# Transposes of z, and of two tiles of the last batch, by 16-bit transfers in a planned attention and feed-forward kernel

## The chip, the cores and the metric

The kernel runs on one core of a Trainium2 chip. The metric is the device time of one execution in microseconds, as the median of several executions. The profile is of one further execution and gives the span from its first to its last instruction.

## What is computed

All data is float32. Eight batches of 512 rows by 256 columns go through two blocks. Cut to what matters:

```python
y  = layernorm(x)
y  = layernorm(y + attention(y, y, y, causal=True)) * g1 + beta1
y  = layernorm(y + attention(y, Z, Z))              * g2 + beta2     # Z: 64 rows of 256 per batch
y  = layernorm(y + relu(y @ w1 + b1) @ w2 + b2)     * g3 + beta3     # w1 256x1024, w2 1024x256
x  = x + y
u  = layernorm(x)
h  = silu(fp4(u) @ fp4(w_gate).T) * (fp4(u) @ fp4(w_up).T)           # 704 columns
x  = x + fp4(h) @ fp4(w_down).T
# fp4: blocks of 16 along the row, scaled by the block's maximum / 6, rounded to a 4-bit grid, scaled back
```

## The kernel before

A batch is four tiles of 128 rows. TensorE contracts over partitions, so y, z, the rounded u (`zq`) and the rounded h must each be turned before a product. There are two ways to turn a tile. By products: TensorE transposes it into a PSUM bank and ScalarE evicts the bank (`transposed`, L411; its transposes are line L419, and L1102 for the last columns of h). By transfers: ScalarE copies the float32 tile into two planes of 16-bit halves (L843 for y, r and zq, L1071 for h), SP writes the planes to DRAM (L849, L1077), and SP issues a transfer that transposes 16-bit elements back into SBUF (L854, L1082). `BY_PRODUCTS` says for which batches y0, r in cross-attention and r in the MLP are turned by products (4, 2 and 1 first batches); zq goes by transfers in every batch, h by transfers in all but the last batch, z by products in every batch.

No engine runs its instructions in program order. Each step is given to a `Plan` with an engine, a duration in microseconds, what it reads and writes, and the buffers that it takes. `Plan.order` runs a small list scheduler over these durations: whenever an engine is free, it takes, from the steps that are ready and whose buffers are free, the one with the least key. The key comes from `DUE`, a table of due times per batch and stage (0 self-attention, 1 cross-attention, 2 MLP, 3 gate and up products, 4 down products), carried back through the successors; `LOAD_EARLY` brings the loads of x and z forward, and `plan.push` moves the weights' rounding. The order that comes out is then emitted, so each engine's queue is fixed, SP's among them. A transfer's `lag` is the planned time from its issue to its landing.

Buffers are kinds with a number of homes (`several(name, count, shape)`); `share` gives a kind a quota out of another kind's homes. The names that matter below:

- `x`, `z`: a batch's inputs, loaded at L358 and L366; `y0`, `r`: the running rows.
- `zT`: the turned z, evicted at L867 with the factor 1/16; it is read at L883 by the products that make the cross-attention's scores, which ScalarE copies to `kq` (L896) and TensorE transposes once more (L900). The products with z as values are L927.
- `turned`: homes of the turned y0, r and zq (evicted at L831 when made by products). `zm`: staging of their 16-bit planes. For zq the same buffer is the mask of the rounding (L578 to L610), held from the maximum on.
- `h` (in `wide`), `hm`, `hqT`: the gated tile, its 16-bit planes, the turned tile; `hd` is the DRAM side. L597 is the absolute value within the rounding, L610 its last step.

The products by line: L767 self-attention scores, L800 its values, L961 and L981 the MLP, L1036 gate and up, L1116 down. L488 are the squares of a layernorm, and L503 and L458 its power -1/2 on POOL. For the last batch all four gated tiles are made first and the four down products follow:

```python
if b == B - 1:
    hs = [gate_up(t) for t in range(NT)]
    for t in range(NT):
        down(t, hs[t])
```

Of the kernel before, what the change touches and what calls it, by code (L numbers as in the profile page):

```python
# [12 lines left out]
U16 = mybir.dt.uint16  # L13
# [6 lines left out]
P = 128  # L20
# [20 lines left out]
TILED = 2.65  # L41

BY_PRODUCTS = (4, 2, 1)
LOAD_EARLY = 2191.0
DUE = [
    [-1877.0, 638.0, 1236.0, -86.0, 359.0],
    [-498.0, 1140.0, 299.0, -53.0, 352.0],
    [251.0, 920.0, -109.0, 452.0, 665.0],
    [2244.0, 599.0, -92.0, 754.0, 95.0],
    [1032.0, 759.0, 1302.0, 1127.0, 22.0],  # L50
    [818.0, -579.0, 119.0, -1108.0, 586.0],
    [771.0, -1583.0, 341.0, 621.0, 85.0],
    [127.0, -388.0, -430.0, -94.0, -1479.0],
    [-2334.0],
]


# [8 lines left out]
def act(cols, bias=False):  # L66
    return 0.06 + cols * 0.84e-3 + 0.19 * bias
# [193 lines left out]
def kernel(  # L261
# [43 lines left out]
    def several(name, count, shape):  # L305
        return [fixed(f"{name}_{k}", shape) for k in range(count)]


    plan = Plan(due=DUE)
    plan.kind("x", several("x", 6, [P, NT, D]))  # L310

    y0_homes = several("y0", 2, [P, NT, D + 2])

    z_homes = several("z", 8, [P, D + 2])
    plan.kind("y0", y0_homes)
    plan.kind("z", z_homes)
    plan.kind("zT", several("zT", 6, [P, ND, SZ]))
    plan.kind("turned", several("turned", 3, [P, ND, S]), ordered=False)
    plan.share("y0T", "turned", 1)
    plan.share("yT", "turned", 3, ordered=False)  # L320
    plan.share("zqT", "turned", 3)
    plan.kind("e", several("e", 1, [P, NT * (NT + 1) // 2 * P]))
    plan.kind("r", several("r", 3, [P, NT, D]))
    plan.kind("kq", several("kq", 4, [P, S // 2]))
    plan.kind("xp", several("xp", 6, [P, NT, SZ]))
    plan.kind("xpT", several("xpT", 3, [P, NT // 2 * P]))
    plan.kind("hT", several("hT", 8, [P, S]))
    plan.kind("zq", several("zq", 1, [P, NT, D]))
    plan.kind("zm", several("zm", 2, [P, NT * D]), ordered=False)
    plan.kind("wide", several("h", 8, [P, NI * P]), ordered=False)  # L330
    plan.share("h", "wide", 5)
    plan.share("hm", "wide", 3)
    plan.share("wq", "wide", 7)
    hqT_homes = several("hqT", 3, [P, NI * P])
    plan.kind("hqT", hqT_homes)

    hd_homes = [dram.tile([P, 2, NI * P], U16, tag=f"hd_{k}", name=f"hd_{k}") for k in range(3)]
# [2 lines left out]
    plan.kind("rest", [rest_home])  # L340
    zd_homes = [dram.tile([NT, P, 2, D], U16, tag=f"zd_{k}", name=f"zd_{k}") for k in range(4)]
    plan.kind("zd", zd_homes, ordered=False)
    plan.kind("ln", several("ln", 12, [P, 48]), ordered=False)
    plan.kind("q", several("q", 6, [P, 3, 64]), ordered=False)
    plan.kind("rt", several("rt", 7, [P, 4]), ordered=False)
    banks = [psum.tile([P, 512], F32, tag=f"bank{k}", name=f"bank_{k}") for k in range(8)]
# [78 lines left out]
    def norm_stats(v, view, pairs):  # L425

        s = plan.buf("ln")

        def st(t):
            return s.ap[:, 6 * t : 6 * t + 6]  # L430

        def mv(t):
            return s.ap[:, 24 + 2 * t : 26 + 2 * t]

        def variances(ts_):
            lo, hi = ts_[0], ts_[-1] + 1
            for t in ts_:
                nc.vector.bn_aggr(mv(t), st(t))
            nc.vector.tensor_scalar(
                s.ap[:, 32 + lo : 32 + hi],  # L440
                s.ap[:, 24:32].rearrange("p (t k) -> p t k", k=2)[:, lo:hi, 1], EPS, None, ALU.add,
            )

        for ts_ in pairs:
            lo, hi = ts_[0], ts_[-1] + 1
            for t in ts_:
                plan.op(
                    "DVE", 0.33, lambda t=t: nc.vector.bn_stats(st(t), view(t)),
                    reads=[(v, t)], writes=[(s, ("st", t))],
                )  # L450
            plan.op(
                "DVE", 0.1 + 0.09 * len(ts_), lambda ts_=ts_: variances(ts_),
                reads=[(s, ("st", t)) for t in ts_],
                writes=[(s, ("var", lo))] + [(s, t) for t in ts_],
            )
            plan.op(
                "POOL", 1.05,
                lambda lo=lo, hi=hi: nc.gpsimd.tensor_tensor(  # L458
                    s.ap[:, 36 + lo : 36 + hi], s.ap[:, 32 + lo : 32 + hi], mhalf[:, lo:hi], ALU.pow
                ),  # L460
                reads=[(s, ("var", lo))], writes=[(s, ("rstd", t)) for t in ts_],
            )
            plan.op(
                "DVE", 0.15,
                lambda lo=lo, hi=hi: nc.vector.scalar_tensor_tensor(
                    s.ap[:, 40 + lo : 40 + hi],
                    s.ap[:, 24:32].rearrange("p (t k) -> p t k", k=2)[:, lo:hi, 0],
                    -1.0, s.ap[:, 36 + lo : 36 + hi], ALU.mult, ALU.mult,
                ),
                reads=[(s, ("rstd", t)) for t in ts_] + [(s, t) for t in ts_],  # L470
                writes=[(s, ("shift", t)) for t in ts_],
            )
        return s

    def sums_stats(v, view, s):


        plan.op(
            "DVE", 0.08,
            lambda: nc.vector.tensor_scalar(  # L480
                s.ap[:, 24:28], s.ap[:, :4], -1.0 / D, None, ALU.mult
            ),
            reads=[(s, ("st", t)) for t in range(NT)], writes=[(s, t) for t in range(NT)],
        )
        for t in range(NT):
            plan.op(
                "ACT", 0.52,
                lambda t=t: nc.scalar.activation(  # L488
                    squares, view(t), AF.Square, bias=s.ap[:, 24 + t : 25 + t],
                    accum_out=s.ap[:, 28 + t : 29 + t],  # L490
                ),
                reads=[(v, t), (s, t)], writes=[(s, ("sq", t))],
            )
        plan.op(
            "DVE", 0.08,
            lambda: nc.vector.tensor_scalar(  # L496
                s.ap[:, 32:36], s.ap[:, 28:32], 1.0 / D, EPS, ALU.mult, ALU.add
            ),
            reads=[(s, ("sq", t)) for t in range(NT)], writes=[(s, "var")],
        )  # L500
        plan.op(
            "POOL", 1.05,
            lambda: nc.gpsimd.tensor_tensor(s.ap[:, 36:40], s.ap[:, 32:36], mhalf, ALU.pow),  # L503
            reads=[(s, "var")], writes=[(s, ("rstd", t)) for t in range(NT)],
        )
# [241 lines left out]
    def self_attention(b, xs):  # L747
# [13 lines left out]
        for k in range(NT):  # L761
            n = S - k * P
            sc = plan.buf("bank")

            def scores(k=k, n=n, sc=sc):
                for c in range(ND):
                    nc.tensor.matmul(  # L767
                        sc.ap[:, :n], yT.ap[:, c, ts(k, P)], yT.ap[:, c, k * P :],
                        start=(c == 0), stop=(c == ND - 1),
                    )  # L770

            plan.op(
                "PE", ND * pe(n), scores, reads=[(yT, c) for c in range(ND)], writes=[sc],
                takes=[e],
            )
            plan.op(
                "ACT", act(n, True),
                lambda k=k, n=n, sc=sc: nc.scalar.activation(

                    e.ap[:, ds(start[k], n)], sc.ap[:, :n], AF.Exp, scale=1.0 / 16.0  # L780
                ),
                reads=[sc], writes=[(e, k)], table="exp",
            )

            plan.op(
                "POOL", 0.35,
                lambda k=k: nc.gpsimd.affine_select(
                    out=e.ap[:, ds(start[k], P)], in_=e.ap[:, ds(start[k], P)],
                    compare_op=ALU.is_ge, fill=0.0, base=0, pattern=[[1, P]],
                    channel_multiplier=-1,  # L790
                ),
                writes=[(e, k)],
            )
# [66 lines left out]
    def cross_attention(b, r, zs):  # L860

        plan.stage = 1
        zT = plan.buf("zT")
        transposed(
            lambda: [zs.ap[:SZ, ts(c, P)] for c in range(ND)], [(zs, 0)], (zT, None),

            lambda pt: nc.scalar.activation(  # L867
                zT.ap, pt[:, : ND * SZ].rearrange("p (c k) -> p c k", c=ND),
                AF.Copy, scale=1.0 / 16.0,
            ),  # L870
            act(ND * SZ), 2,
        )
        yT = turned(r, "yT", b < BY_PRODUCTS[1], lambda t: r.ap[:, t, :])
        sc, nm, xp = plan.buf("bank"), plan.buf("rt"), plan.buf("xp")
# [18 lines left out]

        plan.op("PE", 1.05, products, reads=[yT, zT], writes=[keys])
        kq = plan.buf("kq")
        plan.op("ACT", act(S // 2), lambda: nc.scalar.copy(kq.ap, keys.ap[:, : S // 2]), reads=[keys], writes=[kq])  # L896

        def scores():
            for j in range(2):
# [47 lines left out]
    def mlp(b, r, xs):  # L947
# [8 lines left out]
        for f in range(NF):  # L956
            hp, h = plan.buf("bank"), plan.buf("hT")

            def product(f=f, hp=hp):
# [5 lines left out]

            plan.op("PE", ND * pe(S), product, reads=[yT, ready["w1"]], writes=[hp], takes=[h])
            plan.op(
                "ACT", act(S, True),
                lambda f=f, hp=hp, h=h: nc.scalar.activation(  # L969
                    h.ap, hp.ap, AF.Relu, bias=b1_sb[:, f : f + 1]  # L970
                ),
# [47 lines left out]
    def glu(b, xs, s):  # L1019
# [42 lines left out]
        def down(t, h):  # L1062
            plan.stage = 4
            m = fp4(h, lambda h=h: h.ap[:, :I], "hm", NBI)
            hqT = plan.buf("hqT")
            if b < B - 1:
                hd = plan.buf("hd")
                planes = lambda: m.ap[:, :I].bitcast(U16).rearrange("p (h k) -> p h k", h=2)
                plan.op(
# [65 lines left out]
            )  # L1135


        if b == B - 1:
            hs = [gate_up(t) for t in range(NT)]
            for t in range(NT):  # L1140
                down(t, hs[t])
        else:
            for t in range(NT):
                down(t, gate_up(t))
# [15 lines left out]
        "SP", 5.2, lambda: nc.sync.dma_start(w2_sb, w2.rearrange("(c p) d -> p c d", p=P)),  # L1160
        writes=[ready["w2"]],
    )
    plan.push = 2035.0
    weights()
    plan.push = 0.0
    for b in range(B):
# [38 lines left out]
```

## Time and profile before

| | us |
|---|---|
| median of three executions | 575.2 (574.42, 575.2, 576.3) |
| profiled execution, its own time | 576.26 |
| its span, first to last instruction | 574.5 |
| TensorE busy | 563.8 |
| VectorE busy | 447.8 |
| ScalarE busy | 361.8 |
| POOL busy | 62.2 |

Busy time is the union of an engine's instructions, so pipelined matmuls are not counted twice. The DMA engines were busy 45.4% of the span. In the chain of work that ended last each piece is followed back to what released it; an instruction's line is the line of the helper that emits it, and for transposes the tile's name after `ident` tells what is turned. The granted TensorE clock was 1.00 throughout.

### The profile page before, as it was taken

What the parts mean: (1) busy time and instruction counts of PE and PEld (TensorE: products, weight loads), DVE (VectorE), ACT (ScalarE), POOL (GpSimd) and SP (SyncE); (2) the same over time, 40 slices, a digit from 0 to 9 for tenths busy, and PEclk for the clock granted to TensorE, in tenths of its full rate; (3) what the DMA queues carried; (4) which work ended last, traced back from release to release, by engine and by line L of the source; (5) the groups of instructions that cost most, each with busy time, mean ns of one, the idle gap of its engine ahead of it and who ended that gap; (6) DMA issues with size and microseconds to landing.
All of it is one profiled execution on the core that took longest, in us unless ns stands there. A gap on an engine that the chain in (4) does not pass through costs nothing.

```text
span 574.5 us, 7037 instructions
## 1 busy us (share of the span) xinstructions
PE 563.8 (98%) x2209; PEld 391.2 (68%) x2209; DVE 447.8 (78%) x1125; ACT 361.8 (63%) x761; POOL 62.2 (11%) x93
## 2 busy tenths in 40 slices
PE   5999999999999999999999999999999999999997
PEld 2767584866747668658486667766765866877686
DVE  4789988869998865755259999978997656399892
ACT  4677869598887672791638558887845256364431
POOL 3521101011200120110101102210100000010000
PEclk9999999999999999999999999999999999999999
DMA  7770387246466513322023546585771421436501
GB/s 236 119 230 2 101 219 169 73 119 157 116 158 175 137 52 83 99 71 49 1 73 98 137 126 156 148 198 154 153 180 62 124 62 38 111 106 151 151 19 46
DMA packets 143220, 66.88 MB, mean 116 GB/s; under 512 B 107976, under 2 KB 142672, under 8 KB 143184
## 3 DMA queue, kind: packets, MB, share of 16 engines
q1 hardware_dynamic: 143184, 66.44, 45.4%
q8 instruction: 17, 0.28, 0.2%
q14 instruction: 19, 0.16, 0.1%
HBM read 10.42 MB, written 29.66 MB: 70 GB/s over the span
## 4 chain that ended last, share of the span: by engine, by line
PE 98%; ACT 1%; DMA 0%; SPq 0%; issue 0%; DVE 0%; ACTq 0%
PE bank L1036 27%; PE bank L981 19%; PE bank L961 19%; PE bank L1116 15%; PE bank L767 7%; PE bank L800 6%; PE bank L419 2%; PE bank L927 1%; PE bank L883 1%; DMA z<-in_ctx_dram 0%; ACT squares L488 0%; PE bank L900 0%; SPq L358 0%; ACT turned L831 0%; PE bank L1102 0%
## 5 line engine op out<-in xcount | busy, mean ns | idle before, releaser
L1036 PE MATMUL bank<-wgu,turned 128*128 128x352 f32 x512 | 157.5, 460 | 0.0
L1036 PEld LDWEIGHTS bank<-wgu,turned 128*128 128x128 f32 x512 | 96.3, 190 | 51.8 <-issue 1.7
L981 PE MATMUL bank<-w,hT 128*128 128x256 f32 x512 | 112.6, 379 | 0.0
L961 PE MATMUL bank<-turned,w 128*128 128x512 f32 x256 | 112.5, 593 | 0.0
L981 PEld LDWEIGHTS bank<-w,hT 128*128 128x128 f32 x512 | 97.0, 190 | 13.8
L1116 PE MATMUL bank<-wd,hqT 128*128 128x256 f32 x384 | 87.2, 380 | 0.0
L961 PEld LDWEIGHTS bank<-turned,w 128*128 128x128 f32 x256 | 48.2, 190 | 56.9 <-issue 51.7
L1116 PEld LDWEIGHTS bank<-wd,hqT 128*128 128x128 f32 x384 | 72.4, 190 | 14.2 <-issue 2.9
L503 POOL TENSOR_TENSOR ln<-ln,mhalf 128x4 f32<-128x4 f32 x32 | 37.7, 1180 | 352.0 <-DVE ln L496 352.0
L603 DVE SCALAR_TENSOR_TENSOR h<-h,h 128x704 f32<-128x704 f32 (+2 forms) x76 | 66.8, 883 | 3.8 <-ACT h L597 3.4
L488 ACT ACTIVATE squares<-r,ln 128x256 f32<-128x256 f32 x96 | 48.7, 508 | 32.0 <-DVE ln L480 29.7
L969 ACT ACTIVATE hT<-bank,cols 128x512 f32<-128x512 f32 x64 | 42.8, 681 | 21.7 <-PE bank L961 21.5
L1048 ACT ACTIVATE h<-bank 128x352 f32<-128x352 f32 x64 | 29.2, 460 | 36.4 <-PE bank L1036 32.5
L1071 ACT COPY h<-h 128x1408 uint16<-128x1408 uint16 x28 | 38.0, 1362 | 19.4 <-DVE h L610 17.9
L1055 DVE TENSOR_TENSOR h<-h,bank 128x352 f32<-128x352 f32 x64 | 32.4, 516 | 12.3 <-PE bank L1036 8.6
L992 DVE SCALAR_TENSOR_TENSOR r<-bank,r 128x256 f32<-128x256 f32 x32 | 13.5, 421 | 35.0 <-PE bank L981 34.7
L767 PE MATMUL bank<-turned 128*128 128x512 f32 (+3 forms) x128 | 39.8, 457 | 0.4 <-ACT turned L831 0.4
L597 ACT ACTIVATE h<-h 128x704 f32<-128x704 f32 (+2 forms) x38 | 29.7, 788 | 14.0 <-DVE h L591 13.9
L800 PE MATMUL bank<-y,e 128*128 128x258 f32 x160 | 36.8, 381 | 0.0
L800 PEld LDWEIGHTS bank<-y,e 128*128 128x128 f32 x160 | 30.1, 190 | 5.9 <-issue 1.0
L591 DVE SCALAR_TENSOR_TENSOR h<-h,q 128x704 f32<-128x704 f32 (+2 forms) x38 | 33.5, 883 | 0.2
L610 DVE TENSOR_TENSOR h<-h,q 128x704 f32<-128x704 f32 (+2 forms) x38 | 33.4, 879 | 0.2
(90 smaller groups left out, 639.9 us busy)
## 6 DMA issues: line engine op xcount, KB each, us to landing
zd<-zm SPq DMA_DIRECT2D x25, 512.0 KB, 3.0
hd<-h SPq DMA_DIRECT2D x30, 352.0 KB, 3.0
out_dram<-x SPq DMA_DIRECT2D x32, 128.0 KB, 1.7
x<-in_x_dram SPq DMA_DIRECT2D x7, 512.0 KB, 5.3
w<-in_L_xattn_w_dram SPq DMA_DIRECT2D x2, 1024.0 KB, 7.4
z<-in_ctx_dram SPq DMA_DIRECT2D x16, 64.0 KB, 4.6
zd<-h SPq DMA_DIRECT2D x2, 384.0 KB, 3.1
h<-in_L_ffn_w_down_dram SPq DMA_DIRECT2D x2, 352.0 KB, 4.2
```

Source lines behind the costliest of these rows:

```text
L488: lambda t=t: nc.scalar.activation(squares, view(t), AF.Square, bias=s.ap[:, 24 + t : 25 + t], accum_out=s.ap[:, 28 + t : 29 + t],),
L503: lambda: nc.gpsimd.tensor_tensor(s.ap[:, 36:40], s.ap[:, 32:36], mhalf, ALU.pow),
L591: lambda: nc.vector.scalar_tensor_tensor(blocks_of(view()), blocks_of(view()), TIE, each(rc()), ALU.mult, ALU.mult),
L603: lambda reverse=reverse, f=f: nc.vector.scalar_tensor_tensor(view(), mm(), LEAST, view(), ALU.max, f, reverse1=reverse),
L767: nc.tensor.matmul(sc.ap[:, :n], yT.ap[:, c, ts(k, P)], yT.ap[:, c, k * P :], start=(c == 0), stop=(c == ND - 1),)
L800: nc.tensor.matmul(av.ap[:, : D + 2], e.ap[:, ds(start[k] + (t - k) * P, P)], y0.ap[:, k, :], start=(k == 0), stop=(k == t),)
L961: nc.tensor.matmul(hp.ap, w1_sb[:, c, ts(f, P)], yT.ap[:, c, :], start=(c == 0), stop=(c == ND - 1),)
L969: lambda f=f, hp=hp, h=h: nc.scalar.activation(h.ap, hp.ap, AF.Relu, bias=b1_sb[:, f : f + 1]),
L981: nc.tensor.matmul(fp.ap[:, :D], hT[f].ap[:, ts(t, P)], w2_sb[:, f, :], start=(f == 0), stop=(f == NF - 1),)
L1036: nc.tensor.matmul(gp.ap[:, :HI], zT.ap[:, c, ts(t, P)], wgu[:, c, ds(j * I + n * HI, HI)], start=(c == 0), stop=(c == ND - 1),)
L1071: lambda: nc.scalar.copy(planes(), h.ap[:, :I].bitcast(U16).rearrange("p (k h) -> p h k", h=2)),
L1116: nc.tensor.matmul(op.ap[:, :D], hqT.ap[:, ts(c, P)], wd[:, c, :], start=(c == 0), stop=(c == NI - 1),)
```

## The change

- z is turned by transfers in all batches. ScalarE copies 64 rows of z into two 16-bit planes (`zpl`, five homes), SP writes them to DRAM (`zzd`, four homes) and SP issues the transposing transfer into `zT`. The factor 1/16 moves from the eviction of zT to the copy of `kq`.
- In the last batch, tiles 0 and 1 of h are turned by transfers, as in all other batches; tiles 2 and 3 stay with TensorE.
- Four planned durations take other values: the power on POOL, the squares, the causal selection on POOL and the relu on ScalarE.
- The numbers of homes and quotas change, and the due times, `LOAD_EARLY` and the push of the weights are new. With the durations they set the order of every queue.

```diff
-LOAD_EARLY = 2191.0
+LOAD_EARLY = 5413.0
 DUE = [
-    [-1877.0, 638.0, 1236.0, -86.0, 359.0],
-    [-498.0, 1140.0, 299.0, -53.0, 352.0],
...
+    [-2265.0, 403.0, 787.0, -473.0, 177.0],
+    [-532.0, 884.0, 23.0, -239.0, 262.0],
...
-    plan.kind("x", several("x", 6, [P, NT, D]))
+    plan.kind("x", several("x", 5, [P, NT, D]))
-    z_homes = several("z", 8, [P, D + 2])
+    z_homes = several("z", 6, [P, D + 2])
-    plan.share("y0T", "turned", 1)
+    plan.share("y0T", "turned", 3)
+    plan.kind("zzd", [dram.tile([SZ, 2, D], U16, tag=f"zzd_{k}", name=f"zzd_{k}") for k in range(4)])
+    plan.kind("zpl", several("zpl", 5, [SZ, D]))
-    plan.kind("xp", several("xp", 6, [P, NT, SZ]))
-    plan.kind("xpT", several("xpT", 3, [P, NT // 2 * P]))
-    plan.kind("hT", several("hT", 8, [P, S]))
+    plan.kind("xp", several("xp", 9, [P, NT, SZ]))
+    plan.kind("xpT", several("xpT", 2, [P, NT // 2 * P]))
+    plan.kind("hT", several("hT", 9, [P, S]))
-    plan.kind("zm", several("zm", 2, [P, NT * D]), ordered=False)
-    plan.kind("wide", several("h", 8, [P, NI * P]), ordered=False)
-    plan.share("h", "wide", 5)
+    plan.kind("zm", several("zm", 1, [P, NT * D]), ordered=False)
+    plan.kind("wide", several("h", 7, [P, NI * P]), ordered=False)
+    plan.share("h", "wide", 7)
-    hqT_homes = several("hqT", 3, [P, NI * P])
+    hqT_homes = several("hqT", 5, [P, NI * P])
-    plan.kind("ln", several("ln", 12, [P, 48]), ordered=False)
+    plan.kind("ln", several("ln", 13, [P, 48]), ordered=False)
...
-                "POOL", 1.05,
+                "POOL", 1.12,
-                "ACT", 0.52,
+                "ACT", 0.63,
-                "POOL", 0.35,
+                "POOL", 0.44,
-                "ACT", act(S, True),
+                "ACT", act(S) + 0.08,
...
-        transposed(
-            lambda: [zs.ap[:SZ, ts(c, P)] for c in range(ND)], [(zs, 0)], (zT, None),
-
-            lambda pt: nc.scalar.activation(
-                zT.ap, pt[:, : ND * SZ].rearrange("p (c k) -> p c k", c=ND),
-                AF.Copy, scale=1.0 / 16.0,
+        zpl, zd = plan.buf("zpl"), plan.buf("zzd")
+        halves_ = lambda: zpl.ap.bitcast(U16).rearrange("p (h k) -> p h k", h=2)
+
+        plan.op(
+            "ACT", act(2 * D),
+            lambda: nc.scalar.copy(
+                halves_(), zs.ap[:SZ, :D].bitcast(U16).rearrange("p (k h) -> p h k", h=2)
             ),
-            act(ND * SZ), 2,
+            reads=[(zs, 0)], writes=[zpl],
+        )
+        plan.op(
+            "SP", 0.5, lambda: nc.sync.dma_start(zd.ap, halves_()), reads=[zpl], writes=[zd],
+            takes=[zT], lag=1.5,
+        )
+        plan.op(
+            "SP", 0.6,
+            lambda: nc.sync.dma_start_transpose(
+                zT.ap.rearrange("p c k -> p (c k)").bitcast(U16).rearrange(
+                    "p (c r) -> p c r", c=ND
+                ),
+                zd.ap.rearrange("p h k -> (p h) k"),
+            ),
+            reads=[zd], writes=[zT], lag=TURN,
         )
...
-        plan.op("ACT", act(S // 2), lambda: nc.scalar.copy(kq.ap, keys.ap[:, : S // 2]), reads=[keys], writes=[kq])
+        plan.op("ACT", act(S // 2), lambda: nc.scalar.mul(kq.ap, keys.ap[:, : S // 2], 1.0 / 16.0), reads=[keys], writes=[kq])
...
-            if b < B - 1:
+            if b < B - 1 or t < NT // 2:
                 hd = plan.buf("hd")
...
-    plan.push = 2035.0
+    plan.push = 1992.0
```

More of the change, by code (lines that the diff above doesn't have):

```diff
@@ L43 @@
 BY_PRODUCTS = (4, 2, 1)
-LOAD_EARLY = 2191.0
+LOAD_EARLY = 5413.0
 DUE = [
-    [-1877.0, 638.0, 1236.0, -86.0, 359.0],
-    [-498.0, 1140.0, 299.0, -53.0, 352.0],
[L48 to L54, printed above, removed]
+    [-2265.0, 403.0, 787.0, -473.0, 177.0],
+    [-532.0, 884.0, 23.0, -239.0, 262.0],
+    [-448.0, 675.0, -332.0, 332.0, 652.0],
+    [2530.0, 743.0, -289.0, 375.0, -79.0],
+    [1022.0, 868.0, 1060.0, 1012.0, -159.0],
+    [1336.0, -519.0, 726.0, -1007.0, 912.0],
+    [368.0, -1568.0, 706.0, 983.0, -110.0],
+    [1306.0, -133.0, 648.0, 603.0, -1168.0],
+    [-2659.0],
 ]
@@ L501, in sums_stats @@
         plan.op(
-            "POOL", 1.05,
+            "POOL", 1.12,
             lambda: nc.gpsimd.tensor_tensor(s.ap[:, 36:40], s.ap[:, 32:36], mhalf, ALU.pow),
```

## Prediction

> **What bounds the kernel now.** I read the busy shares and the chain on the page first, then the busy time by stage, what TensorE waited for, and last the chain piece by piece at both ends of the span.
>
> ```profile
> PE 563.8 (98%) x2209; PEld 391.2 (68%) x2209; DVE 447.8 (78%) x1125; ACT 361.8 (63%) x761; POOL 62.2 (11%) x93
> PE 98%; ACT 1%; DMA 0%; SPq 0%; issue 0%; DVE 0%; ACTq 0%
> ```
>
> TensorE is busy for all but 10.7 of 574.5 us and 98% of the chain is its own. By stage (PE busy is the second figure):
>
> ```profile
> 0.00:57.00 57.00, 49.44 (x232) 33.82 (x233) 43.65 (x180) 35.92 (x97) 17.33 (x42) 1.00 0.57 148
> 57.00:531.50 474.50, 474.50 (x1808) 326.95 (x1807) 375.45 (x898) 312.60 (x639) 44.84 (x51) 1.00 0.46 117
> 531.50:575.00 43.50, 39.88 (x173) 30.41 (x171) 28.67 (x49) 13.29 (x27) 0.00 (x0) 0.99 0.26 71
> ```
>
> From 57 to 531 it does not pause at all. Only the first 57 us have waits, and these are they:
>
> ```profile
> PE bank L419 <- DMA z<-in_ctx_dram: 5.6, 1, 5.6
> PE bank L419 <- ACT y L524: 0.9, 1, 0.9
> PE bank L900 <- ACT kq L896: 0.7, 1, 0.7
> PE bank L767 <- ACT turned L831: 0.4, 1, 0.4
> ```
>
> So a microsecond of TensorE work is worth a microsecond, except where the chain runs through another engine. The work to be removed is in two rows of the transposes' line; first and last start are in the row:
>
> ```profile
> L419 PE MATMUL bank<-ident,z x16: 222/247/366, 5.6 to 44.6; 64*128 64x64 f32 x16
> L419 PE MATMUL bank<-ident,h x16: 272/273/273, 555.6 to 565.6; 128*128 128x128 f32 x16
> ```
>
> All z transposes lie in the first 45 us, the very stage with waits. Its chain, and that of the end (start, length, what):
>
> ```profile
> 35.54 0.19 ACT squares L488
> 35.72 0.26 ACT kq L896
> 35.98 0.35 ACT zT L867 x2
> 36.33 0.48 ACT turned L831
> 44.58 0.27 PE bank L419 x2
> ...
> 550.55 5.18 PE bank L1116 x24
> 555.73 0.44 PE bank L419 x4
> 556.17 0.22 PE bank L1102 x2
> 556.39 0.44 PE bank L419 x4
> 556.82 0.22 PE bank L1102 x2
> 557.04 7.77 PE bank L1116 x36
> ```
>
> From 32.3 to 36.8 ScalarE carries the chain; at the end TensorE does.
>
> **Part by part: the z transposes.** Eight pairs leave TensorE. By the timeline they took 0.46 (at 5.56), 0.40 (9.59), 0.31 (21.94), 0.27 (33.45), 0.58 (three pairs at 34.73) and 0.27 (44.58), together 2.29 us. What of it lies on the path? The pair at 5.56 fills the time before y comes from ScalarE (first y transpose at 6.86): 0. At 9.59 the first half of y0T had been evicted by 9.43: 0.40. At 21.94 the eviction that began at 21.61 holds L767 until 22.2: 0. The four pairs at 33.45 and 34.73 lie beside the stretch in which ScalarE is the chain: 0. The pair at 44.58 is in the chain: 0.27. Two zT evictions, 0.35 us, are in the chain on ScalarE at 35.98: 0.35. Sum with the old order: 1.02 us; all of it less the first pair would be 1.83.
>
> **What replaces them.** Per batch: a ScalarE copy of z into 16-bit halves (512 elements a partition: 0.62 by the L843 row) in place of the 0.26 to 0.30 eviction, so 8 x 0.33 = 2.6 us more on an engine that is busy 63% of the first 57 us; a write to DRAM (64 KB: 0.59 of issue by the z loads, 3.0 to landing by the 352 KB hd row); and a transfer that transposes 128 rows (1.23 of issue and 2.5 to landing by the weights' remainder at L688, 128 x 128; 4.0 by the hqT row). A round trip is 6 to 8 us against 0.6. For batch 0, z lands at 5.4, so zT is there by about 14, or 20 with landings of 9 us as the weights had in this stage; L883 first wants it at 33.72. On the chain: nothing; without that cover, 6 to 8 us, once. SP issues 16 more times, 8 x 1.8 = 14.4 us. Behind a transposing transfer that waits for its write stand the x loads, vectors and weights; the one that matters is w1, issued at 28.61, landed by about 36, wanted by L961 at 56.1: cover 20 us, more than 14.4. If every write's 3 us were waited out, 8 x 4.2 = 33.6 us would be 13.6 too late, but z has only six homes, the last two z come after batch 0 and 1 have used theirs, and SP is idle from 37 to 63. I take 0. A ScalarE copy queued before its z has landed (2.1 to 8.8 us by the z loads) would hold the squares and evictions behind it, up to 4 us; again 0, since z was loaded far ahead. The 1/16 moves from the eviction into the kq copy: same instruction count, 0.
>
> **The last batch's first two tiles.** Twelve transposes leave: 0.44+0.22+0.44+0.22 = 1.32 us, all in the chain. ScalarE does a 1.36 copy (L1071) for 0.59+0.27+0.27 of evictions: 0.23 more a tile, ScalarE being under a third busy there. Arrival: tile 0's rounding ends on VectorE at 545.42; copy 1.5, write 3.0, transfer 4.0: 553.9. Tile 1's ends at 550.92; its copy meets L597 of the next tile on ScalarE, so 551 to 552.6; it is there at 559.5 to 561. TensorE, after the gate products end at 550.55, has three products of batch 6 (2.59 each) until 558.3, then tile 0 until 560.9, then tile 1. Tile 0 has 4.4 us of margin, tile 1 1.4 to nothing; doing tile 2's transposes (ready at 556.4) first adds 0.66. If the copy goes ahead of L597, tile 2's rounding is 0.7 later, against 6 us of margin. I take 0 for the wait, bounds 0 and 1.5. If tile 1 waits, batch outputs behind it wait too.
>
> **A rule against it.** The Trainium skill, "VectorE: DVE Perf Modes", "Rules for kernel authors", says to transpose 128x128 on TensorE when a PSUM destination will do, and by DMA otherwise; its section on the transpose paths gives 390 ns against 1309 ns. By that rule the two tiles lose: 8.4 us through DRAM here against 0.66 plus about 1.1 of evictions, +6.6 each, +13 if on the path. The trace has a transpose at 0.11 us of TensorE's time, and covers of 4.4 and about 1 us for the two round trips, so by the trace they gain 1.32. Latency decides only where cover runs out.
>
> **The start's slow matmuls.** L767's 512-wide matmuls run at 1061 to 1220 ns from 9.99 to 13.6, against 592 for L961's, and are normal from about 14, though the granted clock reads 1.00. Does the pair at 5.56 help to warm the array up? "TensorE: Matmul & The Clock Gate", Part 4, says that transposes do not count as busy for the clock; its Part 1 gives about 3.4 us of sustained work. The 4.2 us from 9.99 fit that, the 7.3 from the first y transpose do not. By the rule the removal costs 0; were transposes counted, 1.3 us later warming would cost some 0.65.
>
> **Buffers, durations and dues.** x goes from 6 homes to 5, zm (staging of all 16-bit copies but h and z) from 2 to 1, h to 7, hqT to 5, hT to 9. No row shows what that costs. Below nothing: with true durations (squares at a 0.64 pitch where 0.52 was planned) a better order can win the 0.72 + 0.38 of interior waits and the rest of the z work, some 1.9 us. Above: one hold of the only zm exposed, 6.5 us (below). I take 0, as the nearest row, 474.5 busy of 474.5, shows work always in stock. Extra memsets of hqT pads on POOL: two of 0.2 us, done before the first power at 4.27.
>
> **Sum.** 1.02 + 1.32 = 2.34, say 2.4 us: span 574.5 to 572.1. The profiled execution was 576.26, 1.76 over its span and 1.06 over the median of three, 575.2, near their highest; from the median the forecast is 572.8.
>
> **Rivals.**
> (a) *The start gives its part back.* Four z pairs already lay where ScalarE leads; if the new order leaves as much of a gap, or tile 1 waits its 1.5, 0 to 1.4 us remain: 574.4. For it: the 0.72 and 0.38 waits are in this stage. Against: 0.35 of eviction goes from ScalarE's own chain.
> (b) *Slower: the only staging buffer.* A rounded zq holds zm from its maximum to its write's landing: 511.39 to 526.5, 15.2 us without any hitch, and 54 us between 315.9 and 370 when it had to wait. Eight of these and 17 short uses of about 5.5 us make 216 us, 42% of the stage, and in five stretches of the trace both homes were held (71 to 77, 126 to 131, 156 to 173, 210 to 238, 316 to 370). With one, a y or r waits up to 15.2 us. It decides when TensorE has less than that in stock: an MLP (13.7+13.8) covers it, another batch's self-attention (4.3+4.4) leaves 6.5 us. One such case: 575.2 - 2.4 + 6.5 = 579.3; from 2.4 us exposed on, the kernel is slower. Fewer x homes thin the same stock. Against: five batches still in flight.
> (c) *The work goes but not the time*, since z lies in waits and the tail ends on VectorE: then 575.2. Against: tile 3's rounding ends at 561.58, three us before its transposes at 564.82.
>
> **How the numbers follow.** A measurement can tell about 0.3%, 1.7 us, from no change. The main case 0.56 (571 to 573.9, mostly faster), (a) 0.15, (c) 0.07, (b) 0.22, with like waits of a missing buffer (576 to 580). The range 570.8 to 577.4 leaves out the larger part of (b) and little below.
>
> **What would show it.** Right: no z rows on TensorE, eight h transposes left where 16 were, TensorE about 560 us busy, still no pause from 57 to 531, batch 0's L883 not waiting for DMA. Wrong: a wait of L1116 for a transfer after 550, ScalarE waiting on z loads, zm or x named ahead of idle TensorE in the middle, or a start in which the waits grew by what was removed.

## The result and the profile after

The changed kernel takes 582.93 us (581.22 to 583.63) beside 575.02 us (574.42 to 576.3) for the kernel before: ratio 1.0128, interval 1.0102 to 1.0153. That is 7.4 us slower by this ratio and 7.9 us between the two medians; 572.8 us had been forecast. The execution with the profile took 581.22 us, span 579.5, the shortest of its runs, and that of before was near its longest, so the two profiles show only 5.0 us of it.

Lines have moved: L419 is now L421, L767 L769, L800 L802, L831 L833, L843 L845, L883 L900, L896 L913, L900 L917, L927 L944, L961 L978, L969 L986, L981 L998, L1036 L1053, L1102 L1119, L1116 L1133. In the experiments' kernels lines move by a few in the same way; the text after a fence names the line of before. New are L871 (the copy of z), L877 (its write) and L882 (its transposing transfer).

From the page of the changed kernel, the busy shares and the chain:

```profile
PE 561.7 (97%) x2181; PEld 388.3 (67%) x2181; DVE 446.4 (77%) x1125; ACT 364.2 (63%) x755; POOL 62.5 (11%) x93
PE 89%; ACT 6%; DMA 3%; issue 1%; SPq 1%; POOL 0%; DVE 0%; ACTq 0%
```

The 28 transposes are gone (2209 to 2181), but TensorE is now idle for 17.8 us where it was for 10.7, and a tenth of the chain lies on ScalarE, the DMAs and SP. The busy time by stage of the changed kernel, cut as for before (PE busy is the second figure):

```profile
0.00:57.00 57.00, 46.50 (x214) 32.04 (x214) 42.92 (x166) 40.41 (x104) 18.00 (x45) 1.00 0.55 149
57.00:531.50 474.50, 470.32 (x1780) 321.55 (x1780) 371.53 (x905) 309.36 (x630) 44.47 (x50) 1.00 0.47 117
531.50:580.00 48.50, 44.84 (x190) 34.67 (x189) 31.90 (x56) 14.41 (x23) 0.00 (x0) 1.00 0.40 108
```

Idle TensorE grew from 7.6 to 10.5 us in the first stage and from nothing to 4.2 us in the second; the third lost as little as before. What TensorE waited for (in total, times, longest):

```profile
PE bank L421 <- ACT y L526: 6.3, 1, 6.3
PE bank L900 <- ACT hT L986: 1.6, 1, 1.6
PE bank L944 <- ACT xpT L934: 1.5, 2, 1.0
PE bank L900 <- DMA turned<-zd: 1.3, 1, 1.3
PE bank L802 <- POOL e L789: 0.9, 2, 0.5
PE bank L421 <- ACT xp L907: 0.8, 2, 0.6
PE bank L769 <- ACT turned L833: 0.8, 3, 0.3
PE bank L769 <- DMA turned<-zd: 0.7, 1, 0.7
...
```

The first line is the start, which ends with the first y whatever the order. No other wait is large, but there are a dozen where there were two, most of them for ScalarE. What lies behind them is, for the larger part, the order. Three pieces of TensorE's timeline in the kernel before (start, length, what): batch 0's first cross-attention product, its first MLP product, and the first of the second MLP matrix.

```profile
33.72 1.08 PE L883 MATMUL bank<-turned,zT 128*64 128x256 f32 x8
56.10 13.90 PE L961 MATMUL bank<-turned,w 128*128 128x512 f32 x32
71.14 5.13 PE L981 MATMUL bank<-w,hT 128*128 128x256 f32 x23
```

The same in the changed kernel, with the idle time before a piece in brackets:

```profile
41.90 1.08 PE L900 MATMUL bank<-turned,zT 128*64 128x256 f32 x8
59.30 14.00 PE L978 MATMUL bank<-turned,w 128*128 128x512 f32 x32 [0.34 <-ACT turned L833]
74.85 1.08 PE L900 MATMUL bank<-turned,zT 128*64 128x256 f32 x8 [1.55 <-ACT hT L986]
```

At 14.70 us the changed kernel began its first L802 product, 1.9 us ahead of before (16.62). Its cross-attention then starts 8.2 us later, and nothing waits at 41.90: that is simply where the plan put it, behind the third batch of self-attention products. The MLP starts 3.2 us later. SP's queue shows how late z came (start, length, what):

```profile
20.59 0.43 SPq L1174 DMA_DIRECT2D w<-in_L_xattn_w_dram  x1
21.06 0.47 SPq L1178 DMA_DIRECT2D w<-in_L_xattn_w_dram  x1
21.63 7.20 SPq L877 DMA_DIRECT2D zzd<-zpl  x4
34.23 5.15 SPq L882 DMA_TRANSPOSE zT<-zzd  x4
```

The copy of z for batch 0 was done at 5.7, but its write stands behind the vectors and both 1 MB matrices, at 21.63; it took up to 12.6 us to land behind them, and the transposing transfer went out at 34.23. Whether this late place or the new due times put the cross-attention where it stands, no run parts. From 44.7 to 74.8 us ScalarE carries nearly the whole chain; some pieces of it around 60 us:

```profile
56.59 1.54 ACT zm L845 x3
58.13 0.64 ACT h L599
58.77 0.35 ACT turned L833
59.12 4.03 DMA zd<-zm
63.17 0.62 ACT zm L845
...
73.56 1.28 ACT hT L986 x2
74.85 1.08 PE bank L900 x8
```

The end did what was forecast. Its chain in the changed kernel has the transposes of two tiles where there were four, and no wait of L1133 for a transfer:

```profile
554.31 7.77 PE bank L1133 x36
562.08 0.44 PE bank L421 x4
562.51 0.22 PE bank L1119 x2
562.73 7.77 PE bank L1133 x36
```

### The profile page after: what moved, and what is told of

Same layout as the page of the kernel before. It is cut to its first block, busy times and chain, and to the rows that moved or that the text cites. A ratio compares the mean times of both kernels' runs of the same rounds, so it can differ in the third digit from the quotient of the medians.

```text
span 579.5 us, 6999 instructions
## 1 busy us (share of the span) xinstructions
PE 561.7 (97%) x2181; PEld 388.3 (67%) x2181; DVE 446.4 (77%) x1125; ACT 364.2 (63%) x755; POOL 62.5 (11%) x93
## 4 chain that ended last, share of the span: by engine, by line
PE 89%; ACT 6%; DMA 3%; issue 1%; SPq 1%; POOL 0%; DVE 0%; ACTq 0%
PE bank L1053 25%; PE bank L998 19%; PE bank L978 17%; PE bank L1133 14%; PE bank L802 6%; PE bank L769 4%; DMA turned<-zd 2%; ACT squares L490 2%; PE bank L900 1%; PE bank L944 1%; PE bank L421 1%; ACT turned L833 1%; ACT hT L986 1%; ACT zm L845 1%; DMA zd<-zm 1%
## 5 line engine op out<-in xcount | busy, mean ns | idle before, releaser
L1053 PE MATMUL bank<-wgu,turned 128*128 128x352 f32 x512 | 156.3, 460 | 0.0
L1053 PEld LDWEIGHTS bank<-wgu,turned 128*128 128x128 f32 x512 | 96.2, 190 | 52.4 <-issue 2.6
L978 PE MATMUL bank<-turned,w 128*128 128x512 f32 x256 | 113.1, 594 | 0.3 <-ACT turned L833 0.3
L998 PE MATMUL bank<-w,hT 128*128 128x256 f32 x512 | 113.1, 380 | 0.0
L998 PEld LDWEIGHTS bank<-w,hT 128*128 128x128 f32 x512 | 96.9, 190 | 14.5 <-issue 1.2
L1133 PE MATMUL bank<-wd,hqT 128*128 128x256 f32 x384 | 86.5, 379 | 0.0
L978 PEld LDWEIGHTS bank<-turned,w 128*128 128x128 f32 x256 | 48.1, 190 | 55.3 <-issue 50.4
L1133 PEld LDWEIGHTS bank<-wd,hqT 128*128 128x128 f32 x384 | 72.6, 190 | 14.1 <-issue 2.9
L505 POOL TENSOR_TENSOR ln<-ln,mhalf 128x4 f32<-128x4 f32 x32 | 39.2, 1226 | 338.3 <-DVE ln L498 338.3
L986 ACT ACTIVATE hT<-bank,cols 128x512 f32<-128x512 f32 x64 | 42.9, 686 | 16.4 <-PE bank L978 16.3
L1088 ACT COPY h<-h 128x1408 uint16<-128x1408 uint16 x30 | 40.9, 1363 | 16.8 <-DVE h L612 12.6
L769 PE MATMUL bank<-turned 128*128 128x512 f32 (+3 forms) x128 | 38.0, 445 | 1.5 <-ACT turned L833 0.8
L802 PE MATMUL bank<-y,e 128*128 128x258 f32 x160 | 37.2, 382 | 0.9 <-POOL e L789 0.9
L802 PEld LDWEIGHTS bank<-y,e 128*128 128x128 f32 x160 | 29.8, 190 | 6.8 <-POOL e L789 1.3
L769 PEld LDWEIGHTS bank<-turned 128*128 128x128 f32 x128 | 22.8, 193 | 16.3 <-issue 8.3
```

Source lines behind the costliest of these rows:

```text
L769: nc.tensor.matmul(sc.ap[:, :n], yT.ap[:, c, ts(k, P)], yT.ap[:, c, k * P :], start=(c == 0), stop=(c == ND - 1),)
L802: nc.tensor.matmul(av.ap[:, : D + 2], e.ap[:, ds(start[k] + (t - k) * P, P)], y0.ap[:, k, :], start=(k == 0), stop=(k == t),)
L978: nc.tensor.matmul(hp.ap, w1_sb[:, c, ts(f, P)], yT.ap[:, c, :], start=(c == 0), stop=(c == ND - 1),)
L986: lambda f=f, hp=hp, h=h: nc.scalar.activation(h.ap, hp.ap, AF.Relu, bias=b1_sb[:, f : f + 1]),
L998: nc.tensor.matmul(fp.ap[:, :D], hT[f].ap[:, ts(t, P)], w2_sb[:, f, :], start=(f == 0), stop=(f == NF - 1),)
L1053: nc.tensor.matmul(gp.ap[:, :HI], zT.ap[:, c, ts(t, P)], wgu[:, c, ds(j * I + n * HI, HI)], start=(c == 0), stop=(c == ND - 1),)
```

## The experiments

Two theories stood against each other. One: the plan draws a new order as soon as a step, a duration, a due time or a home changes, and this order, not the transfers, costs the time. The other: the transfers themselves cost it (the write's landing, the only `zm`, SP's queue). To price a step without the plan's answer to it, the runs called "held" let the plan order the steps of the kernel before, take the transposes out of the finished list, and put the transfers in at fixed places (the edit is shortened; z's planes, their DRAM side and the two more turned tiles of h have buffers of their own there):

```diff
-    for _, o in plan.order():
-        o.emit()
+    steps = [(w, o.emit) for w, o in plan.order() if o not in gone]   # gone: transposes and evictions
+    steps += transfers                                                # (time in the plan, emit)
+    for _, emit in sorted(steps, key=lambda s: s[0]):
+        emit()
```

**Tiles alone, order held.** Tiles 0 and 1 of the last batch by transfers: copy 1.0 us after the plan's time of the last rounding step, write 2.4 and transfer 5.5 after it.

> The order before held; only the last batch's tiles 0 and 1 go by transfers. Theory A: 1.3 us faster (1.32 us of transposes out of TensorE's tail, both turned tiles there in time). Theory B: L1116 of tile 1 waits for its transfer, up to 1.5 us, so no gain or a small loss.

573.95 us, ratio 0.9978 (0.9972 to 0.9984): 1.3 us faster. The chain's end in this kernel:

```profile
550.29 12.95 PE bank L1123 x60
563.24 0.44 PE bank L421 x4
563.68 0.22 PE bank L1108 x2
```

Sixty down products (L1123 is L1116) follow each other without a pause, where before the transposes of two tiles came between them. This is the only step that brings time, and this version beats both kernels.

**z alone, order held.** Z_AT gives the plan's times of copy, write and transfer.

```diff
+    Z_AT = [(8.75, 10.6, 17.15), (10.5, 11.9, 17.16)] + [
+        (60.0 + 3 * k, 61.5 + 3 * k, 66.0 + 3 * k) for k in range(6)
+    ]
```

> The order of all other instructions is that of the kernel before; only z goes by transfers, batch 0's write and transposing transfer standing on SP before the pads and vectors. Theory A (the loss is in the new order, not in the transfers): as the prediction's working had it for the old order, 0.5 to 1.8 us faster than before, no z rows on TensorE, first 57 us with at most 1 us more idle TensorE. Theory B (the round trips themselves are the loss): L883 of batch 0 waits for zT or the start of another engine is held, 3 us or more slower than before.

578.96 us, ratio 1.0069 (1.0057 to 1.0081). That is the loss which the second theory expected, though not by its wait: batch 0's z came in time. The MLP began at 54.75 instead of 56.10, but most of these 1.35 us are not the missing transposes: the first sixteen products of self-attention took 5.51 us here and 6.79 in the profile of before, and their length varies from 5.2 to 6.8 us over the profiles, with z's transposes and without. A part of what was lost stands in the chain:

```profile
80.92 0.53 SPq L1189
...
81.50 4.58 DMA turned<-zd
...
86.12 1.08 PE bank L888 x8
```

The six later z (L1189 is their write) stood on SP ahead of the transposing transfer of r (`turned<-zd`), and TensorE waited at L888, the L883 of before, 2.35 us for that one; it also waited 1.9 us for `kq`, where it was 0.7. So SP's time does have a price: not on w1, whose cover the prediction had counted, but on other turned tiles.

**z alone, order held, places improved.** First the later z in stretches where SP was idle (held_z2), then the first two writes behind the x loads with their transfers behind the vectors as well (held_z3):

```diff
-        (8.75, 10.6, 17.15), (10.5, 11.9, 17.16), (46.0, 47.8, 52.0), (48.0, 50.0, 55.0),
-        (107.0, 107.8, 110.5), (108.0, 108.6, 110.8), (109.0, 118.5, 122.5), (110.0, 119.0, 123.5),
+        (8.75, 17.15, 27.05), (10.5, 17.16, 27.06), (46.0, 47.8, 52.0), (48.0, 50.0, 55.0),
+        (107.0, 116.6, 120.0), (108.0, 117.0, 121.0), (109.0, 118.5, 122.5), (110.0, 119.0, 123.5),
```

> As held_z (the order before, only z by transfers), with the round trips of batches 2 to 7 moved to stretches in which SP stands idle in the trace of before (two at 47 to 55 us, four at 107 to 124) instead of 61 to 85, where held_z's turned transfer came 2.4 us late for L888. If SP's queue was held_z's loss: the first MLP product still at about 54.8 us, no wait of L888 for a transfer at 86, and 1 to 2 us faster than before. If the copies on ScalarE or the transfers as such cost time: no faster than before.

> As held_z2, with the first two batches' writes behind the x loads and their transposing transfers behind the vectors on SP, ahead of w1, and the later ones at 117 to 124 us; in the trace of held_both2 the vectors, issued 3.4 us later than before because a transfer that transposes waits on SP for its write, came at 31.9 us and held VectorE and with it the kq copy. If SP's serial queue is what eats the gain at the start: the wait for kq falls from 2.8 us back towards 0.7, and the kernel is 0.5 to 2 us faster than before. If z's transposes only filled gaps of TensorE: that wait stays at 1.3 us or more, and the time is that of before within 1 us.

577.83 us (1.0037, 1.0022 to 1.0052), then 576.08 us (1.0014, 1.0006 to 1.0022); a gain of 1 to 2 us had been expected of the first. In the second the MLP begins at 53.24, 2.9 us ahead of before (1.0 of it again in the first sixteen products), and the time is still no better. TensorE's waits in it:

```profile
PE bank L422 <- ACT y L528: 6.1, 1, 6.1
PE bank L905 <- ACT kq L901: 1.5, 1, 1.5
PE bank L888 <- DMA turned<-zd: 0.9, 1, 0.9
```

The wait for `kq` (L905 is L900) has doubled from 0.7, and a new one comes later. In held_z2, where the vectors stood on SP behind the first z's transfers and one landed only at 32.06 and held VectorE, that wait was 2.3 us, and the granted clock fell to 0.51 behind it. The profiled run was the shortest of this kernel (574.9), so its page doesn't show where the whole of the start's lead went. At the best of the places tried, z's turning by transfers gains nothing.

**Both steps, order held**, with z placed as in held_z2 and as in held_z3:

> Both replacements in the order before: held_z2 and held_tiles together. If their gains add up: held_z2's gain plus 1.3 us, so some 2.3 to 3.3 us faster than before; that would be the prediction's 2.34 us, without the new order.

> held_z3 and held_tiles together: held_z3's change plus 1.3 us of gain. Faster than both kernels (572 to 574) if held_z3 gains or is even; if the later stages are tied to transfers that do not come earlier (turned zq at 122, turned y at 367), no better than held_tiles alone.

576.99 us (1.0026, 1.0015 to 1.0037) and 574.71 us (0.9992, 0.9983 to 1.0001): each 0.8 to 1.4 us under its own z alone. The changed kernel's two steps can thus be had for the old time: 574.71 us in the order and with the homes of before, 582.93 in the new plan, some 8 us for the same steps. With the tiles alone it is a little less still.

**Batch 0's z late, order held.** As held_z, with its write behind the vectors, w1 and w2 on SP (the loads of w1 and w2 are put at 31.0, ahead of it), and TensorE's order untouched:

```diff
-    Z_AT = [(8.75, 10.6, 17.15), (10.5, 11.9, 17.16)] + [
+    Z_AT = [(8.75, 31.3, 31.8), (10.5, 11.9, 17.16)] + [
...
+    big = (ready["w1"], ready["w2"])
+    steps = [(31.0 if o.engine == "SP" and o.bufs[0] in big else w, o.emit) for w, o in plan.order() if not any(o in st[:2] for st in z_steps)]
```

> As held_z, but batch 0's write and transposing transfer stand on SP behind the vectors, w1 and w2, where the changed kernel has them; TensorE's order is that of before, so L883 of batch 0 stays at its place. If the late place on SP is what makes zT late: zT lands 8 to 14 us after TensorE wants it at about 32 us, and the time is 6 to 12 us over held_z. If transfers land in time wherever they stand: as held_z.

592.58 us, ratio 1.0286 (1.0263 to 1.0309). Two pieces of TensorE's timeline (L888 is L883, L771 L767), two of SP's queue, and two stretches (granted clock is the third figure from the end) of this kernel:

```profile
44.08 1.97 PE L888 MATMUL bank<-turned,zT 128*64 128x256 f32 x8 [12.36 <-DMA zT<-zzd]
47.01 3.78 PE L771 MATMUL bank<-turned 128*128 128x512 f32 x4
```

```profile
34.05 0.59 SPq L1189 DMA_DIRECT2D zzd<-zpl  x1
41.60 1.21 SPq L1194 DMA_TRANSPOSE zT<-zzd  x1
```

```profile
32.00:44.00 12.00, 0.00 (x0) 0.00 (x0) 3.40 (x11) 2.25 (x8) 1.51 (x1) 0.63 0.64 200
44.00:52.00 8.00, 7.44 (x21) 3.97 (x22) 4.69 (x13) 4.50 (x12) 0.45 (x1) 0.50 0.42 132
```

The late z costs 13.6 us against held_z when TensorE's order does not give way: a wait of 12.4, and products at half clock after it (1.97 for eight that take 1.08, 3.78 for four that take 1.98); 6 to 12 us had been expected. This z is later than the changed kernel's: nine loads of z held SP for 10.3 us ahead of the weights, so the transposing transfer left at 41.60 and not at 34.23. With the changed kernel's zT, there at 36.5, the old order would have waited some 3 to 5 us (an estimate from the reader's place at 32.05 in held_z and 33.72 before). In the changed kernel the third batch's self-attention stands in this place, and TensorE does not wait.

**The changed kernel without z's turning.** All its planned steps, durations, dues and homes, but z's copies, writes and transfers are not issued; zT holds a constant, so this part of the computation is left out.

```diff
-            lambda: nc.sync.dma_start(zd.ap, halves_()), reads=[zpl], writes=[zd],
+            lambda: None, reads=[zpl], writes=[zd],
...
```

> The changed kernel, every queue in its own order, with the turning of z left out altogether (no copy, write or transfer; zT holds a constant). Theory A: it is still 4 us or more slower than before, since batch 0's cross-attention keeps its late place in TensorE's queue; 0 to 2 us faster than the changed kernel (copies off ScalarE). Theory B: close to the kernel before or faster, within 1 us.

580.08 us, ratio 1.0084 (1.0071 to 1.0097): 4.8 us slower than before, although z costs nothing at all in it and TensorE has 28 transposes less to do. Of TensorE's timeline in this kernel:

```profile
42.49 1.08 PE L895 MATMUL bank<-turned,zT 128*64 128x256 f32 x8
59.66 14.00 PE L973 MATMUL bank<-turned,w 128*128 128x512 f32 x32 [0.24 <-ACT turned L836]
```

The cross-attention (L895 is L883) and the MLP (L973 is L961) start as late as in the changed kernel. So the order, with the homes that go with it, carries at least 4.8 of the 7.4 us (both by the ratios), and z's steps within this order about 2.6. From the windows of the profiles, TensorE's idle time in us:

| | 0 to 57 | 57 to 75 | 75 to 531 | 531 to the end |
|---|---|---|---|---|
| before | 7.6 | 0 | 0 | 3.1 |
| changed, without z's turning | 9.6 | 0.6 | 2.1 | 3.2 |
| changed | 10.5 | 2.2 | 2.0 | 3.2 |

The 2 us of the middle are the order's (two waits for turned transfers), as is most of the start; what z's steps add shows between 57 and 75, where ScalarE is the chain. Idle time is not all: the same 2181 products kept TensorE busy for 561.7 us in the changed kernel and 560.0 in held_both3, and no run explains these 1.7 us.

**A second staging buffer.** The changed kernel and its order, but the transfers use two homes of `zm` in turn.

> The changed kernel, every queue in its own order, but the staging buffer zm has two homes taken in turn. Theory C (rival b of the prediction, the only staging buffer, is the loss): ScalarE's waits for the write out of zm (6.6 us in the changed kernel's trace) go and the time falls by 4 us or more. Theory A: those waits go, but the time falls by 0 to 2 us, since ScalarE's work and the order around it stay.

582.9 us, ratio 1.0135 (1.0122 to 1.0148): no different. In the changed kernel ScalarE waited for the only buffer as the prediction's rival (b) had it:

```profile
ACT zm L845 <- DMA zd<-zm: 6.6, 4, 2.5
```

With two homes this row is gone from ScalarE's waits, and the time stays; TensorE's wait at 75 us, 1.6 for `hT` before, is 1.9 for the copy into `zm` itself. Rival (b)'s mechanism falls.

**The changed kernel with tiles 0 and 1 back on TensorE**, planned anew:

```diff
-            if b < B - 1 or t < NT // 2:
+            if b < B - 1:
```

> The changed kernel with tiles 0 and 1 of the last batch turned by TensorE again, all else as changed; the planner's order differs only at the end. If the tiles' transfers gain in the changed kernel too: 1 to 1.6 us slower than the changed kernel. If they cost there (L1133 waiting): equal or faster.

582.62 us, ratio 1.0134 (1.0118 to 1.015), beside the changed kernel's 1.0128 (1.0102 to 1.0153). The two can't be told apart, where 1 to 1.6 us of difference had been expected; whether the tiles bring their 1.3 us in this order is not settled.

**The plan's inputs one at a time**, in the kernel before. Only the four durations (`durations`); only the homes and quotas (`homes`); only `DUE`, `LOAD_EARLY` and the push (`dues`); and z's steps alone, planned with the old inputs (`z_planned`).

> Before with the four planned durations of the change and nothing else: no transfer changes, the due times are the old ones. If the due times fit only the durations they were made with: the order falls apart and the time rises by 4 to 12 us, idle TensorE in the first 150 us. If better durations alone give a better order: 0.5 us faster or more.

> The kernel before with only the changed numbers of homes and quotas (x 5, z 6, zm 1, xp 9, xpT 2, hT 9, h 7, hqT 5, ln 13, the two shares); z and the tiles stay on TensorE, durations and dues as before. Theory: the list scheduler draws a new order whenever anything that it weighs changes, and dues fitted to the old set then serve it badly: slower by 8 to 20 us, with TensorE's waits spread over the first 75 us, the middle and the end, hardly any of them on zm or x. Rival (the prediction's step): a buffer costs only where its hold is exposed, 0 to 6.5 us, in one or two waits that name zm or x.

> The kernel before with only the new due times, LOAD_EARLY and push; nothing else changed. Theory: due times are good for one set of steps, durations and homes; the new ones without their set are worse than the old ones: slower by 15 to 60 us, most of it idle TensorE in the middle, with every instruction the same as before. Rival: the dues bring the better order themselves, so alone they cost under 3 us or gain up to 1.9.

> z by transfers alone, the order made anew by the planner from the old due times, old durations and old homes (five homes for the planes added). If the order that comes out is the loss: 8 to 14 us slower than before, much of it as idle TensorE before 75 us, with batch 0's first MLP product at 60 us or later. If the planner adapts: within 2 us of held_z.

| | us | ratio (interval) |
|---|---|---|
| durations | 585.05 | 1.0173 (1.0147 to 1.0198) |
| homes | 598.78 | 1.0416 (1.0393 to 1.0439) |
| dues | 645.69 | 1.1226 (1.1205 to 1.1248) |
| z_planned | 590.15 | 1.0268 (1.0249 to 1.0288) |

The first three have TensorE execute the same 2209 products as before, and lose 10, 24 and 71 us, the homes and the dues more than had been expected (8 to 20 and 15 to 60). The longest waits of TensorE after the start with the homes alone:

```profile
PE bank L1036 <- DMA turned<-zd: 8.6, 1, 8.6
...
PE bank L1116 <- DMA hqT<-hd: 3.2, 2, 2.5
PE bank L961 <- DVE h L603: 2.6, 1, 2.6
```

and with the dues alone:

```profile
PE bank L1116 <- ACT hqT L1095: 11.0, 1, 11.0
PE bank L961 <- DMA turned<-zd: 8.7, 1, 8.7
PE bank L419 <- DVE h L610: 7.8, 1, 7.8
```

None names `zm` or `x`; one with the homes alone follows a step of `h`, whose homes change too (8 to 7, its quota 5 to 7). The 8.6 is the last batch's turned zq, whose rounding the order let finish at 541 on VectorE between steps of the gated tiles. A scarce home can also act through the order that the plan draws with it, and these runs don't part the two. The new dues are no better order in themselves. With their own set of steps they seem to make up for much, since z planned with the old inputs costs 14.8 us and the whole change 7.9; no run shows this by itself. The pieces do not add up, as each draws another order. Dues fitted to the new steps with z's writes ahead of the weights were not tried.

## Why the prediction was wrong, point by point

- **"Buffers, durations and dues": taken as 0, and this is the step that failed.** The same steps took 574.71 us in the old order and 582.93 in the new one, and even without z's turning the new order was 4.8 us over the kernel before; each input alone cost 10 to 71. How much of this is the order and how much the fewer homes acting within it is not parted, but for `zm`, which was worth nothing. The reason given, that 474.5 of 474.5 busy "shows work always in stock", read a result as a reserve: that row belongs to one order, and the change replaces the order. The bound above, 6.5 us for one exposed hold of `zm`, was a bound on a buffer and not on an order.
- **SP's cost, taken as 0, was wrong.** The transposing transfer's issue was sized well (1.2 us), but the cover was sought at w1. What stood behind z's transfers were other turned tiles (2.35 us in held_z) and the vectors (held_z2), and what stood ahead of batch 0's z were the constants and 2 MB of weights: its landing took up to 12.6 us where 3, or at worst 9, were allowed. "About 14, or 20" for zT became 36.5 in the changed kernel (34.23 of start, 2.3 to landing). TensorE did not wait for it only because the plan had moved its reader from 33.72 to 41.90. The price without cover, "6 to 8 us, once", was 13.6 in held_z_late, where zT came later still and the clock fell.
- **1.02 us from z's transposes: not there.** With the order held, z cost 0.8 us at its best place (ratio 1.0014) instead of gaining 1.02. The start did get shorter, by up to 2.9 us at the first MLP product, of which 1.0 us lies in the slow first products. The traces show part of it given back, in waits for `kq` (0.8 us more) and for a turned tile (0.9), as rivals (a) and (c) had it for the start; where the rest went is open.
- **1.32 us from the two tiles: right,** 1.3 with the order held. Here the trace also decided rightly against the Trainium skill's rule ("VectorE: DVE Perf Modes", "Rules for kernel authors") that prefers TensorE: the covers of the two round trips held, and L1123 did not wait.
- **The slow first matmuls, taken as 0: no price was seen.** The sixteen products of L769 took 5.47 us in the changed kernel and 6.84 in the same order without z's turning, with no z transposes in either, and 6.79 before, so the transposes don't set it. The Trainium skill, "TensorE: Matmul & The Clock Gate", Part 1, says that the clock's window runs freely of the kernel's start, which would make it a matter of chance; no run here shows the window itself.
- **Rival (b), 579.3 us, came nearest and was wrong in its cause**: ScalarE's waits on `zm` were there, and taking them away changed nothing. (Its 216 us are 46% of the 474.5-us stage, not 42%.)
- **The signs to look for** did their work: TensorE's 561.7 us of busy time (about 560 forecast) and batch 0's product not waiting for a DMA came as for a right forecast, and the pauses between 57 and 531, with a start whose waits grew by more than was removed, showed it wrong.

## What to carry to other kernels

Where queues are filled by a list scheduler with fitted due times, the unit of change is the order: before counting removed instructions, lay the new order beside the old one and see which steps have moved past which, on the serial DMA queue first. To learn what a step is worth, hold the old order and put the step into it by hand; only the part that still gains there (here the two tiles at the end) is worth planning anew. A full engine says that its order fits, not that work lies in reserve.

## What the runs showed of the hardware that was not expected

- A late transfer can be paid twice, as a long wait slows the products behind it too. Behind the wait of 12.4 us TensorE's granted clock was 0.50 until about 52 us (held_z_late); behind one of 3.3 us in z_planned it was 0.51. Waits of 2.2 to 2.8 us went both ways: behind 2.22 us (held_z_late), 2.33 (held_z2) and 2.63 (homes) the clock fell to about 0.5 within 4 us, behind 2.35 us (held_z) and 2.78 (held_both2) it stayed at 1.00. The changed kernel's waits of up to 1.6 us after its start left it at 1.00. The Trainium skill, "TensorE: Matmul & The Clock Gate", Part 1, gives about 3.4 us of idleness for this; here shorter waits were enough in some cases, and the measurement decides.
- A 64 KB write issued right behind two loads of 1 MB landed after up to 12.6 us in the changed kernel and after 7.5 in held_z_late; the shortest of the same writes took 2.0 us in the changed kernel.
